# A two-layer decoder on one core: first attention in a fixed TensorE order, norms by powers on GpSimd, and later or earlier turns for experts and gated layer

## The chip, the core and the metric

The kernel runs on one NeuronCore of a Trainium2 chip. TensorE (PE) does matmuls and transposes, VectorE (DVE), ScalarE (ACT) and GpSimd (POOL) the rest, SyncE (SP) issues most of the transfers. The metric is the device time of one execution in microseconds (us); lower is better.

## The reference

The input is x, 16 sequences of 128 tokens with 256 features, and a context of the same shape. Two layers, each of three residual blocks on a layer norm of x:

```python
# layer 0
x = x + attention(ln(x))          # 16 heads of 128, causal, softmax
x = x + wkv(ln(x), ctx)           # a recurrence over the tokens, by channel
h = ln(x)                         # 16 experts of width 176, the top 4 of softmax(h @ router.T)
x = x + sum_top4(w_e * (silu(h@G_e) * (h@U_e)) @ D_e) + sigmoid(h@s) * shared(h)
# layer 1
x = x + rms_attention(ln(x))      # 16 heads of 16
x = x + cross_attention(ln(x), ctx)   # 16 query heads of 128 over 4 key heads
q = act_quant(ln(x))              # rounded to 127 steps of each row's largest
h = silu(q @ tern(Wg).T) * (q @ tern(Wu).T)
x = x + act_quant(h) @ tern(Wd).T # "gated layer": weights of -1, 0, 1; 832 wide
```

## The kernel before

Rows of 128 tokens are called tiles; four tiles make a group g. x stays in SBUF throughout. PE, DVE, ACT and POOL each work through a queue in order. Which instruction stands where in a queue is set by the program's order and by a planner that may reorder within its bounds; inside a `manual_schedule(engines={ET})` PE's own order is the program's.

**First attention** (8 to 648 us). A unit is one tile and four heads: 64 units. `pipeline` runs a step per unit with the stages `scores` (scores `sc`, the causal mask by a POOL affine select, `projv`, the softmax), `values` two steps later (`z`), `ahead` (the q and k projections `proj` of the next four heads; the norm of the next group, `norm0`), `project_out` three steps later (`acc_l`), `turn` one step later (`pT`, and its copy `probT`). The fifth stage, `between`, issues up to two waiting scatters and takes four turns of the generator `wkv_and_route`: when a group's attention is done, its wkv block and routing run in pieces beside the next group's units. A `yield` ends a piece. wkv takes the norm of four tiles (`norm_stats`, `norm_T`: the rows `hrow`, eight transposes `lnT`), works on the two halves of the features with DVE scans, ACT exponentials and POOL products, and adds its result to x by transposes `addb`. `route` takes the norm `hg`, the logits, the top four, and a place in the expert's list `hs` in DRAM; 16 POOL scatters per group (`scatter`) write the rows there. The last group's wkv and route run beside the shared expert.

**Shared expert** (650 to 784 us): 24 units of `pg`, `pu`, `acc_sh`.

**Routed experts** (784 to 1055 us): 79 tiles of 128 list rows. Per step s the loop issues `fetch(s)`, `turn_in(s-2)` (transposes `pht`), `inner(s-3)` (`pgu`, and on DVE `eact`), `turn_act(s-4)` (transposes `pat`, copied by DVE to `eactT`), `outer(s-LAG)` (`pey`, written back to `hs`), and `beside(s)`: loads, the rounding of the gated layer's weights, the gathers of finished rows, and from step FIRST on the first pieces of layer 1. `pht`, `pgu`, `pat` and `pey` share the PSUM pool `tps` with four buffers.

**Layer 1** (1055 us to the end): 64 slots, four to a batch of one tile, in a manual PE order. Each step u issues `scores(u)`, `query_sums(u+1)`, `pieces(early)`, `project_out(u-3)`, `query_norms(u+1)`, `values(u-2)`, `project(u+2)`, `pieces(late)`, `turn(u-1)`, `pieces(last)`. The tables early, late and last name by slot which pieces of the first layer-1 attention (`sa_...`, up to six batches ahead) and of the gated layer (`ff_...`, batches behind) go there. The gated layer's pieces are `ff_start` (norm and rounding, `xqq`), `ff_first_T` (`xqpT`), `inner0` and `inner1` (`pg`, `pu`, the hidden rows `hh`, and after inner1 the rounding to `hqq`), `ff_second_T` (`hqpT`) and `ff_outer` (`py`, the result to DRAM). `ends` and the final loop place those of the last batches.

**Norms.** In layer 0 1/sqrt is an ACT Sqrt and a DVE reciprocal (`rsqrt`); in layer 1 it is a POOL power with the exponent -0.5 (`power`).

Of the kernel before, what the change touches and what calls it, by code (L numbers as in the profile page):

```python
# [17 lines left out]
P = 128  # L18
B = 16
# [33 lines left out]
def decoder(ctx, tc, a, out):  # L53
# [58 lines left out]
    V.memset(zeros_b, 0.0)  # L112
    eps = {}
    for e in (LN_EPS, ATT_EPS, RMS_EPS):
        eps[e] = const.tile([P, 1], F32, tag=f"eps{len(eps)}", name=f"eps{len(eps)}")
        V.memset(eps[e], e)
    warm = const.tile([P, 1], F32, name="warm")
    A.activation(warm, eps[LN_EPS], AF.Sqrt)

# [3 lines left out]

    def rsqrt(pool, src, shape, eps_, tag, scale=1.0):
        r = pool.tile(list(shape), F32, tag=tag, name=tag)
        A.activation(r, src, AF.Sqrt, bias=eps[eps_], scale=scale)
        V.reciprocal(r, r)
        return r

    def norm_stats(pool, g):  # L130
        st = pool.tile([P, G, 6], F32, tag="bnst", name="bnst")
        mv = pool.tile([P, G, 2], F32, tag="bnmv", name="bnmv")
        for t in range(G):
            V.bn_stats(st[:, t, :], xt[g * G + t])
            V.bn_aggr(mv[:, t, :], st[:, t, :])
        return mv, rsqrt(pool, mv[:, :, 1], [P, G], LN_EPS, "rstd")

    def norm_rows(pool, g, t, mv, scale, bufs=2):
        h = pool.tile([P, D], F32, tag="hrow", name="hrow", bufs=bufs)
        V.tensor_scalar(h, xt[g * G + t], mv[:, t, 0:1], scale[:, t : t + 1], ALU.subtract, ALU.mult)  # L140
        return h

    def norm_T(pool, g, mv, scale, dst, bufs=2, psum="main"):

        pts = [ps4("lnT", psum) for _ in range(NK)]
        for t in range(G):
            h = norm_rows(pool, g, t, mv, scale, bufs)
            for k in range(NK):
                PE.transpose(pts[k][:, t, :], h[:, k * P : (k + 1) * P], ident)
        for k in range(NK):  # L150
            nc.any.tensor_copy(dst(k), pts[k])

    def layernorm_T(pool, g, bufs=2, psum="main"):
        hT = pool.tile([P, NK, GT], F32, tag="hT", name="hT")
        mv, rstd = norm_stats(pool, g)
        norm_T(pool, g, mv, rstd, lambda k: hT[:, k, :].rearrange("p (t s) -> p t s", t=G), bufs, psum)
        return hT

# [10 lines left out]
    def heads_out(acc, t, zT, w, h0, last):  # L169
# [6 lines left out]
        return ins.ins  # L176

    def add_back(g, yT, gate=None):

        for t in range(G):  # L180
            pb = ps1("addb")
            for k in range(NK):
                PE.transpose(pb[:, k * P : (k + 1) * P], yT[:, k, t * S : (t + 1) * S], ident)
            x = xt[g * G + t]
            if gate is None:
                V.tensor_tensor(x, x, pb[:, :D], ALU.add)
            else:
                V.scalar_tensor_tensor(x, pb[:, :D], gate[:, t : t + 1], x, ALU.mult, ALU.add)

# [63 lines left out]
    behind = []  # L253

    def wkv(g, psum):

# [6 lines left out]
        yield  # L263
        norm_T(wkp, g, mv, rstd, lambda k: kp[k][:, :, 1:], 2, psum)
        yield
        for k in range(NK):
# [51 lines left out]
            V.tensor_tensor(y, aa0, bb0, ALU.mult)  # L318
            for _ in range(5):
                yield  # L320
            pb = ps4("addb", psum)
# [78 lines left out]
    def route(g, psum):  # L400
# [10 lines left out]
        hg = rt.tile([P, G, D], F32, tag="hg", name="hg")  # L411
        pts = [ps4("lnT", psum) for _ in range(NK)]
        yield
        for t in range(G):
            V.tensor_scalar(hg[:, t, :], xt[g * G + t], mv[:, t, 0:1], rstd[:, t : t + 1], ALU.subtract, ALU.mult)
            for k in range(NK):
                PE.transpose(pts[k][:, t, :], hg[:, t, k * P : (k + 1) * P], ident)
        yield
        hT = rt.tile([P, NK, GT], F32, tag=f"hT{g}", name=f"hT{g}")
        for k in range(NK):  # L420
            nc.any.tensor_copy(hT[:, k, :].rearrange("p (t s) -> p t s", t=G), pts[k])
        routed_T[g] = hT
        yield
        plg = pools[psum].tile([P, G, 32], F32, tag="ps", name="plg")
# [59 lines left out]
        gtb = small("gtb", [P, G, E], BF16)  # L484
        V.tensor_copy(gtb, gt)
        pc = pools[psum].tile([P, 2, G, E], F32, tag="ps", name="pcnt")
        for j, w in ((0, "before"), (1, "ones_b")):
# [51 lines left out]
    with tc.tile_pool(name="l0", bufs=2, reuse_waits="tile") as wk0:  # L539
        hTs, qTs, kTs, live, accs = {}, {}, {}, {}, {}  # L540
        side, last_pool = [], []
# [9 lines left out]

        def norm0(g):
            hTs[g] = layernorm_T(wk0, g, 2, "side")

# [36 lines left out]
        def ahead(u):  # L591

            g, hq, t = place(u)
            if hq == NQ - 2 and t == 0 and g + 1 < NG:
                with tc.issue_after(softmax.last):
                    norm0(g + 1)
            if hq == 0 and t == 2:
                add_bias(g)
            if (u // G + 1) < NG * NQ:
                project(*place(u + G)[:2], t)  # L600
# [32 lines left out]

        norm0(0)
        bias_rows()
        for i in range(4):
            project(0, 0, i)
        pipeline(
            NG * NQ * G,
            [(scores, 0), (values, 2), (ahead, 0), (project_out, 3), (turn, 1), (between, 0)],  # L640
        )
    psum0.close()
# [82 lines left out]

    ET, SPE = mybir.EngineType.PE, mybir.EngineType.SP
    why = "the map holds each of its candidates once"
# [224 lines left out]
    U = B * NKV  # L952
    mhalf = xa.tile([P, 2 * H], F32, name="mhalf")
    GP.memset(mhalf, -0.5)

    def power(v, n):

        power.last = GP.tensor_tensor(v, v, mhalf[:, :n], ALU.pow).ins  # L958

    def flat2(v):  # L960
# [193 lines left out]

    hurried = {}

    def pieces(table, u):
        b, n = divmod(u, NKV)
        for f, ahead in table[n]:
            if 0 <= b + ahead < B - hurried.get(f, 0):  # L1160
                f(b + ahead)
# [19 lines left out]

    LAG, FIRST, APART = 5, 35, 2
    GATHER = TOPK + E - 1 + LAG + 2
# [302 lines left out]
    hurried.update({ff_start: 2, ff_first_T: 2, inner0: 2, inner1: 2, ff_second_T: 3, ff_outer: 3})  # L1486
# [7 lines left out]
    def unit(f, u):  # L1494
        if 0 <= u < U:
            f(u)


# [4 lines left out]
    with tc.manual_schedule(engines={ET}):  # L1503
        keys(0)
        project(0)
        project(1)
        query_sums(0)
        values_in(0)
        query_norms(0)
        keys_T(0)  # L1510
        keys(1)
        for u in range(U + 3):
            unit(scores, u)
            unit(query_sums, u + 1)
            pieces(early, u)
            unit(project_out, u - 3)
            unit(query_norms, u + 1)
            unit(values, u - 2)
            unit(project, u + 2)
            pieces(late, u)  # L1520
            unit(turn, u - 1)
            pieces(last, u)
            for f, n in ends.get(u, ()):
                f(B - n)
# [45 lines left out]
```

## Time and profile before

| What | us |
|---|---|
| median of 3 runs | 1710.32 (1708.59 to 1715.99) |
| the profiled execution | 1719.15 |
| its span | 1717.5 |
| PE busy | 1635.2 |
| DVE busy | 957.8 |
| ACT busy | 839.2 |
| POOL busy | 546.6 |
| PE clock, mean | 0.984 |

A span is the time from the first to the last instruction of the profiled execution. Rows give an engine, the source line, the operation with its tiles (out<-in), and the idle time ahead of it with what ended that. POOL's powers of layer 1 are at line 958, the Sqrt of layer 0 at line 126; the layer-0 scatters are at line 520.

### The profile page before, as it was taken

The page shows a single profiled execution, that of the slowest core. Times are in us where ns is not written, and L with a number is a line of the kernel's source. Part 1 is how long each engine was busy: PE and PEld are TensorE (multiplying, and loading weights), DVE is VectorE, ACT ScalarE, POOL GpSimd, SP SyncE. Part 2 cuts the span into 40 slices and gives each one's busy share as a digit, 9 for nine tenths or more (in the row PEclk, how much of TensorE's full clock was granted, in tenths as well). Part 3 has the DMA queues.
Part 4 walks back from the last instruction along what each step waited for, and adds up shares of the span by engine and source line. Part 5 has one row for each costly group of instructions (what it writes and reads, how often), then busy time and mean ns, then how long its engine had stood idle before and what let it go on. Part 6 is the DMA issues. An engine that isn't in the chain of part 4 may idle for free.

```text
span 1717.5 us, 27384 instructions
## 1 busy us (share of the span) xinstructions
PE 1635.2 (95%) x9824; PEld 1149.0 (67%) x9824; DVE 957.8 (56%) x2522; ACT 839.2 (49%) x2229; POOL 546.6 (32%) x554
## 2 busy tenths in 40 slices
PE   8999999999998988999999999899999999999995
PEld 4666656656665665556676667677777777777773
DVE  2333675375538457613345555467666666666664
ACT  4454545455444534212434445565665666555552
POOL 1010221241124042211146345644444444323320
PEclk9999999999999999999999999999999999999996
DMA  9990000000000019213353235000000000000000
GB/s 294 396 344 1 1 13 1 31 25 7 6 32 25 1 50 251 82 40 102 111 151 116 93 91 171 28 4 8 7 8 7 8 7 10 7 8 7 4 7 10
DMA packets 91646, 110.24 MB, mean 64 GB/s; under 512 B 8630, under 2 KB 66934, under 8 KB 91510
## 3 DMA queue, kind: packets, MB, share of 16 engines
q1 hardware_dynamic: 83078, 89.55, 16.0%
q0 software_dynamic: 6144, 16.79, 3.2%
q10 hardware_dynamic: 2288, 2.14, 0.4%
q8 instruction: 79, 1.29, 0.3%
q14 instruction: 57, 0.47, 0.1%
HBM read 54.06 MB, written 54.39 MB: 63 GB/s over the span
## 4 chain that ended last, share of the span: by engine, by line
PE 78%; issue 7%; DVE 7%; POOL 4%; ACT 3%; DMA 1%; POOLq 0%; ACTq 0%; DVEq 0%; SPq 0%
PE proj L563 11%; PE proj L1309 6%; PE acc_x L1374 6%; PE projv L582 5%; PE acc_l L172 5%; PE pgu L912 4%; PE pey L935 3%; PE sc L1339 3%; PE z L611 3%; PE sc L573 3%; PE z L1359 3%; PE pg L698 2%; PE acc_sh L716 2%; PE pu L698 2%; PE pkv L1051 1%
## 5 line engine op out<-in xcount | busy, mean ns | idle before, releaser
L199 ACT ACTIVATE sc<-sc,nmax 128x128 f32<-128x128 f32 x512 | 199.2, 390 | 183.9 <-DVE nmax L196 150.4
L196 DVE TENSOR_REDUCE nmax<-sc 128x4 f32<-128x512 f32 x128 | 87.3, 682 | 191.6 <-POOL sc L576 188.4
L576 POOL TENSOR_SCALAR_AFFINE_SELECT sc<-sc 128x512 f32<-128x512 f32 x64 | 42.9, 670 | 378.1 <-ACT sc L575 352.3
L1309 PEld LDWEIGHTS proj<-hc,wbig 128*128 128x128 f32 x1024 | 125.3, 194 | 34.0 <-issue 22.0
L1309 PE MATMUL proj<-hc,wbig 128*128 128x128 f32 x1024 | 126.2, 277 | 4.2 <-DVE sc L1342 3.9
L958 POOL TENSOR_TENSOR rq<-rq,mhalf 128x4 f32<-128x4 f32 x64 | 66.8, 1043 | 194.9 <-DVE rq L1332 178.8
L582 PE MATMUL projv<-wv,hT 128*128 128x512 f32 x256 | 123.1, 603 | 5.9 <-DVE v L587 4.6
L1374 PE MATMUL acc_x<-wbig,zT 128*128 128x256 f32 x512 | 126.0, 389 | 0.0
L563 PE MATMUL proj<-hT,wq 128*128 128x512 f32 x256 | 124.7, 609 | 0.0
L172 PE MATMUL acc_l<-wo,zT 128*128 128x256 f32 x512 | 121.6, 380 | 0.0
L172 PEld LDWEIGHTS acc_l<-wo,zT 128*128 128x128 f32 x512 | 96.4, 190 | 37.4 <-issue 27.1
L563 PE MATMUL proj<-hT,wk 128*128 128x512 f32 x256 | 121.0, 593 | 0.0
L912 PE MATMUL pgu<-wbig,hxT 128*128 x316 | 109.6, 470 | 4.5 <-DVE eactT L928 3.2
L1374 PEld LDWEIGHTS acc_x<-wbig,zT 128*128 128x128 f32 x512 | 94.2, 192 | 23.1 <-issue 11.3
L958 POOL TENSOR_TENSOR ss<-ss,mhalf 128x32 f32<-128x32 f32 x16 | 87.1, 5442 | 43.8 <-DVE ss L1060 43.8
L1342 DVE SCALAR_TENSOR_TENSOR sc<-sc,rq,mask 128x128 f32<-128x128 f32 x256 | 77.9, 342 | 35.9 <-PE sc L1339 21.4
L611 PEld LDWEIGHTS z<-probT,v 128*128 128x128 f32 x512 | 67.5, 194 | 44.1 <-issue 26.2
L199 ACT ACTIVATION_READ_ACCUMULATOR sc<-sc,nmax 128x1 f32 x512 | 95.7, 187 | 0.0
L1169 POOL DMA_INDIRECT back<-hs,idx x64 | 63.6, 993 | 93.3 <-DMA hs<-ey 75.5
L563 PEld LDWEIGHTS proj<-hT,wk 128*128 128x128 f32 x256 | 48.4, 191 | 59.4 <-issue 50.3
L928 DVE COPY eactT<-pat 88x256 f32<-88x256 f32 x79 | 33.0, 418 | 91.7 <-PE pat L926 68.1
L1345 POOL TENSOR_TENSOR sc<-sc,rsum 128x512 f32<-128x512 f32 x64 | 66.9, 1046 | 50.0 <-DVE rsum L1344 18.6
(352 smaller groups left out, 3538.6 us busy)
## 6 DMA issues: line engine op xcount, KB each, us to landing
hs<-zero SPq DMA_DIRECT2D x16, 2048.0 KB
hx<-hs SPq DMA_DIRECT2D x79, 128.0 KB
hs<-ey SPq DMA_DIRECT2D x79, 128.0 KB
wbig<-in_L_ffn_w_gate_dram SPq DMA_DIRECT2D x2, 1408.0 KB
wbig<-in_L_ffn_w_up_dram SPq DMA_DIRECT2D x2, 1408.0 KB
wd<-in_L_ffn_w_down_dram SPq DMA_DIRECT2D x2, 1408.0 KB
x<-in_x_dram SPq DMA_DIRECT2D x4, 512.0 KB
wq<-in_L_attn_W_Q_dram SPq DMA_DIRECT2D x8, 256.0 KB
```

The lines of the kernel that those rows point to most:

```text
L172: ins = PE.matmul(acc[:, t, :], zT[:, i, :], w[:, h0 + i, :], start=False, stop=last and i == 3, skip_group_check=True,)
L196: softmax.last = V.tensor_reduce(nmax, sc, AX.X, ALU.max, negate=True).ins
L199: A.activation(p[:, i, :], sc[:, i, :], AF.Exp, bias=nmax[:, i : i + 1], accum_out=rs[:, i : i + 1])
L563: PE.matmul(pj, w[:, k, h, :], hTs[g][:, k, :], start=k == 0, stop=k == NK - 1)
L582: PE.matmul(pv, hTs[g][:, k, at], wv[:, k, 4 * hq : 4 * hq + 4, :].rearrange("p h e -> p (h e)"), start=k == 0, stop=k == NK - 1,)
L611: PE.matmul(pz[:, i, :], v[:, i, :], pT[:, i, :], start=True, stop=True)
L698: ins = PE.matmul(d[c * HP : c * HP + cols.stop - cols.start, :n], w[:, k, cols], routed_T[g][:, k, c * n : (c + 1) * n], start=k == 0, st ...
L912: PE.matmul(pg, hT[:, k, :], wgu[:, k, bass.ds(held[j], 1), :].rearrange("p e i -> p (e i)"), start=k == 0, stop=k == NK - 1,)
L958: power.last = GP.tensor_tensor(v, v, mhalf[:, :n], ALU.pow).ins
L1309: PE.matmul(pj[:, i, :], wqx[:, n, k, i * DH : (i + 1) * DH], hTs[b][:, k, :], start=k == 0, stop=k == NK - 1,)
L1342: V.scalar_tensor_tensor(sc[:, i, :], psc[:, i, :], rq[:, i : i + 1], mask, ALU.mult, ALU.add)
L1374: PE.matmul(accs[b][:, :D], zT[:, i, :], wox[:, 4 * n + i, :], start=n == 0 and i == 0, stop=n == NKV - 1 and i == 3,)
```

## The change

- PE's order in first attention is that of the program. `norm0` is spread over three steps; `hrow` has four buffers.
- `rsqrt` goes; `norm_stats` uses a DVE add and `power`.
- The generator takes four turns (`a_unit`) between wkv's rows and their transposes, between route's rows and their transposes, between those and the logits, and ahead of the counts `pcnt`; four instead of five ahead of `addb`.
- Experts: `turn_act` at lag 5, LAG 6, FIRST 36.
- Gated layer: ff_start in slot 2 (was 3), ff_first_T in 3 (was 0 of the next batch), inner0 in 0 (was 1), inner1 in 1 (was 2), ff_second_T in 2 (was 0 of the next batch), ff_outer in 3 (was 1 of the next batch). The pieces of batch 14 are placed in the last steps by the stage that they follow, and those of batch 15 and the last ff_outer calls behind the loop.

```diff
-    def rsqrt(pool, src, shape, eps_, tag, scale=1.0):
-        r = pool.tile(list(shape), F32, tag=tag, name=tag)
-        A.activation(r, src, AF.Sqrt, bias=eps[eps_], scale=scale)
-        V.reciprocal(r, r)
-        return r
+    def power(v, n):
+        power.last = GP.tensor_tensor(v, v, mhalf[:, :n], ALU.pow).ins
...
-        return mv, rsqrt(pool, mv[:, :, 1], [P, G], LN_EPS, "rstd")
+        r = pool.tile([P, G], F32, tag="rstd", name="rstd")
+        V.tensor_scalar_add(r, mv[:, :, 1], LN_EPS)
+        power(r, G)
+        return mv, r
...
+    def a_unit():
+        for _ in range(4):
+            yield
...
-        norm_T(wkp, g, mv, rstd, lambda k: kp[k][:, :, 1:], 2, psum)
+        hs = norm_rows(wkp, g, mv, rstd)
+        yield from a_unit()
+        norm_T(hs, lambda k: kp[k][:, :, 1:], psum)
...
-            for _ in range(5):
-                yield
+            yield from a_unit()
             pb = ps4("addb", psum)
...
-            if hq == NQ - 2 and t == 0 and g + 1 < NG:
+            if hq == NQ - 2 and t < 3 and g + 1 < NG:
                 with tc.issue_after(softmax.last):
-                    norm0(g + 1)
+                    norm0(g + 1, t)
...
-        pipeline(
-            NG * NQ * G,
-            [(scores, 0), (values, 2), (ahead, 0), (project_out, 3), (turn, 1), (between, 0)],
-        )
+        with tc.manual_schedule(engines={ET}):
+            pipeline(
+                NG * NQ * G,
+                [(scores, 0), (values, 2), (ahead, 0), (project_out, 3), (turn, 1), (between, 0)],
+            )
...
-    LAG, FIRST, APART = 5, 35, 2
+    LAG, FIRST, APART = 6, 36, 2
...
-                for f, lag in ((fetch, 0), (turn_in, 2), (inner, 3), (turn_act, 4), (outer, LAG)):
+                for f, lag in ((fetch, 0), (turn_in, 2), (inner, 3), (turn_act, 5), (outer, LAG)):
...
-        [(load_context, 2), (norm_rows_x, 1), (keys_T, 1), (ff_first_T, -2), (ff_second_T, -3)],
-        [(norm_T_x, 1), (inner0, -2), (ff_outer, -3)],
-        [(values_in, 1), (inner1, -2)],
-        [(row_stats, 2), (ff_start, -1)],
+        [(load_context, 2), (norm_rows_x, 1), (keys_T, 1), (inner0, -2)],
+        [(norm_T_x, 1), (inner1, -2)],
+        [(values_in, 1), (ff_second_T, -2), (ff_start, -1)],
+        [(row_stats, 2), (ff_outer, -2), (ff_first_T, -1)],
...
     ends = {
-        U - 2: [(ff_start, 2)],
-        U - 1: [(ff_second_T, 3), (ff_first_T, 2), (inner0, 2), (ff_outer, 3), (inner1, 2)],
-        U: [(ff_second_T, 2)],
-        U + 1: [(ff_outer, 2)],
+        (U - 1, "turn"): [ff_start],
+        (U, "project_out"): [ff_first_T, inner0],
+        (U, "values"): [inner1],
+        (U + 1, "values"): [ff_second_T],
     }
...
-        for f in hurried:
+        for f in (ff_start, ff_first_T, inner0, inner1):
             f(B - 1)
+        ff_outer(B - 2)
+        ff_second_T(B - 1)
+        ff_outer(B - 1)
```

More of the change, by code (lines that the diff above doesn't have):

```diff
@@ L112, in decoder @@
     V.memset(zeros_b, 0.0)
[L113 to L118, printed above, removed]
+    mhalf = const.tile([P, 2 * H], F32, name="mhalf")
+    GP.memset(mhalf, -0.5)
+    ET, SPE = mybir.EngineType.PE, mybir.EngineType.SP
     tdecay = vector_load("L0_xattn_time_decay", [P, NK])
     tfirst = vector_load("L0_xattn_time_first", [P, NK])
-    def rsqrt(pool, src, shape, eps_, tag, scale=1.0):
-        r = pool.tile(list(shape), F32, tag=tag, name=tag)
-        A.activation(r, src, AF.Sqrt, bias=eps[eps_], scale=scale)
-        V.reciprocal(r, r)
-        return r
+    def power(v, n):
+        power.last = GP.tensor_tensor(v, v, mhalf[:, :n], ALU.pow).ins
     def norm_stats(pool, g):
@@ L135, in norm_stats, with norm_rows, norm_T, by_tiles @@
             V.bn_aggr(mv[:, t, :], st[:, t, :])
-        return mv, rsqrt(pool, mv[:, :, 1], [P, G], LN_EPS, "rstd")
[L138 to L143, printed above, removed]
+        r = pool.tile([P, G], F32, tag="rstd", name="rstd")
+        V.tensor_scalar_add(r, mv[:, :, 1], LN_EPS)
+        power(r, G)
+        return mv, r
+    def norm_rows(pool, g, mv, scale):
+        hs = []
+        for t in range(G):
+            h = pool.tile([P, D], F32, tag="hrow", name="hrow", bufs=G)
+            V.tensor_scalar(h, xt[g * G + t], mv[:, t, 0:1], scale[:, t : t + 1], ALU.subtract, ALU.mult)
+            hs.append(h)
+        return hs
+    def norm_T(hs, dst, psum):
         pts = [ps4("lnT", psum) for _ in range(NK)]
         for t in range(G):
-            h = norm_rows(pool, g, t, mv, scale, bufs)
             for k in range(NK):
-                PE.transpose(pts[k][:, t, :], h[:, k * P : (k + 1) * P], ident)
+                PE.transpose(pts[k][:, t, :], hs[t][:, k * P : (k + 1) * P], ident)
         for k in range(NK):
             nc.any.tensor_copy(dst(k), pts[k])
[L153 to L157, printed above, removed]
+    def by_tiles(hT, k):
+        return hT[:, k, :].rearrange("p (t s) -> p t s", t=G)
     def rows_accumulator(name):
@@ L176, in heads_out @@
         return ins.ins
[L178 to L188, printed above, removed]
     def last_dim(v, n):
@@ L411, in route @@
         hg = rt.tile([P, G, D], F32, tag="hg", name="hg")
-        pts = [ps4("lnT", psum) for _ in range(NK)]
         yield
@@ L415, in route @@
             V.tensor_scalar(hg[:, t, :], xt[g * G + t], mv[:, t, 0:1], rstd[:, t : t + 1], ALU.subtract, ALU.mult)
-            for k in range(NK):
-                PE.transpose(pts[k][:, t, :], hg[:, t, k * P : (k + 1) * P], ident)
-        yield
+        yield from a_unit()
         hT = rt.tile([P, NK, GT], F32, tag=f"hT{g}", name=f"hT{g}")
-        for k in range(NK):
-            nc.any.tensor_copy(hT[:, k, :].rearrange("p (t s) -> p t s", t=G), pts[k])
+        norm_T([hg[:, t, :] for t in range(G)], lambda k: by_tiles(hT, k), psum)
         routed_T[g] = hT
-        yield
+        yield from a_unit()
         plg = pools[psum].tile([P, G, 32], F32, tag="ps", name="plg")
@@ L485, in route @@
         V.tensor_copy(gtb, gt)
+        yield from a_unit()
         pc = pools[psum].tile([P, 2, G, E], F32, tag="ps", name="pcnt")
@@ L539, in decoder @@
     with tc.tile_pool(name="l0", bufs=2, reuse_waits="tile") as wk0:
-        hTs, qTs, kTs, live, accs = {}, {}, {}, {}, {}
+        hTs, qTs, kTs, live, accs, norms = {}, {}, {}, {}, {}, {}
         side, last_pool = [], []
@@ L550, in bias_rows, with norm0 @@
             V.tensor_copy(bo_row, pb[:, :D])
-        def norm0(g):
-            hTs[g] = layernorm_T(wk0, g, 2, "side")
+        def norm0(g, part):
+            if part == 0:
+                norms[g] = norm_stats(wk0, g)
+            elif part == 1:
+                norms[g] = norm_rows(wk0, g, *norms[g])
+            else:
+                hTs[g] = wk0.tile([P, NK, GT], F32, tag="hT", name="hT")
+                norm_T(norms.pop(g), lambda k: by_tiles(hTs[g], k), "side")
         def add_bias(g):
@@ L632, in between @@
                     side.pop(0)
-        norm0(0)
+        for part in range(3):
+            norm0(0, part)
         bias_rows()
@@ L724, in sh_down @@
                 V.scalar_tensor_tensor(xt[b], acc[:, t, :], sg[:, b : b + 1], xt[b], ALU.mult, ALU.add)
-    ET, SPE = mybir.EngineType.PE, mybir.EngineType.SP
     why = "the map holds each of its candidates once"
@@ L952, in decoder @@
     U = B * NKV
[L953 to L958, printed above, removed]
     def flat2(v):
@@ L1153, in decoder @@
     last = ([(row_stats, 6)], [(sa_scale, 6)], [(sa_rows, 6), (sa_split, 5)], [])
-    hurried = {}
+    apart = {}
     def pieces(table, u):
@@ L1159, in pieces @@
         for f, ahead in table[n]:
-            if 0 <= b + ahead < B - hurried.get(f, 0):
+            if 0 <= b + ahead < B - apart.get(f, 0):
                 f(b + ahead)
@@ L1485, in decoder, with unit @@
     early[3].append((keys, 2))
-    hurried.update({ff_start: 2, ff_first_T: 2, inner0: 2, inner1: 2, ff_second_T: 3, ff_outer: 3})
+    for f in (ff_start, ff_first_T, inner0, inner1, ff_second_T, ff_outer):
+        apart[f] = 2
     ends = {
-        U - 2: [(ff_start, 2)],
-        U - 1: [(ff_second_T, 3), (ff_first_T, 2), (inner0, 2), (ff_outer, 3), (inner1, 2)],
-        U: [(ff_second_T, 2)],
-        U + 1: [(ff_outer, 2)],
+        (U - 1, "turn"): [ff_start],
+        (U, "project_out"): [ff_first_T, inner0],
+        (U, "values"): [inner1],
+        (U + 1, "values"): [ff_second_T],
     }
-    def unit(f, u):
+    def unit(f, u, step=None):
         if 0 <= u < U:
             f(u)
+        for f_ in ends.get((step, f.__name__), ()):
+            f_(B - 2)
     late_backs = {
@@ L1515, in decoder @@
             pieces(early, u)
-            unit(project_out, u - 3)
+            unit(project_out, u - 3, u)
             unit(query_norms, u + 1)
-            unit(values, u - 2)
+            unit(values, u - 2, u)
             unit(project, u + 2)
             pieces(late, u)
-            unit(turn, u - 1)
+            unit(turn, u - 1, u)
             pieces(last, u)
-            for f, n in ends.get(u, ()):
-                f(B - n)
             if u in late_backs:
```

## The prediction

> **What bounds the kernel now.** The page first: TensorE (PE) is busy for 95% of the span and DVE for 56%, so the time is PE's work plus the holes in it. The second line shows that PE ran at full clock except in a few slices, above all the last.
>
> ```profile
> PE 1635.2 (95%) x9824; PEld 1149.0 (67%) x9824; DVE 957.8 (56%) x2522; ACT 839.2 (49%) x2229; POOL 546.6 (32%) x554
> ...
> PEclk9999999999999999999999999999999999999996
> ```
>
> Then the windows by stage (length, PE, weight loads, DVE, ACT, POOL, clock, DMA): first attention, shared expert, routed experts, steady gated layer, end.
>
> ```profile
> 8.00:648.00 640.00, 617.73 (x2728) 401.98 (x2728) 332.60 (x691) 309.65 (x833) 139.26 (x168) 0.99 0.23 80
> 650.00:784.00 134.00, 127.99 (x478) 72.53 (x477) 68.36 (x148) 35.83 (x50) 29.40 (x33) 0.99 0.40 111
> 784.00:1055.00 271.00, 255.26 (x1545) 184.56 (x1544) 130.78 (x364) 115.21 (x293) 107.84 (x95) 0.99 0.39 122
> 1106.00:1548.00 442.00, 441.78 (x3763) 346.64 (x3761) 294.50 (x912) 267.82 (x734) 193.35 (x164) 1.00 0.02 7
> 1662.00:1717.50 55.50, 33.30 (x158) 20.51 (x156) 28.40 (x87) 17.79 (x43) 4.17 (x5) 0.75 0.03 10
> ```
>
> First attention lacks 22.3 us, the routed experts 15.7, the end 22.2; the steady gated layer lacks 0.2 in 442: there the change can only lose. Third, what PE waits for (total, times, longest):
>
> ```profile
> PE hqpT L1409 <- ACT hqq L847: 12.8, 3, 4.9
> PE z L611 <- ACT probT L212: 10.8, 8, 2.1
> ...
> PE pat L926 <- DVE eact L919: 5.6, 6, 2.0
> PE xqpT L1409 <- ACT xqq L847: 4.7, 1, 4.7
> PE projv L582 <- DVE v L587: 4.6, 1, 4.6
> ...
> PE pgu L912 <- DVE eactT L928: 3.2, 2, 2.5
> ```
>
> PE's work is the same in both kernels, so I price holes. A hole also costs clock: after the 2.07 us wait of z at 391.5 the window 392.6 to 396.0 shows clock 0.51, so 3.4 us do 1.7 us of work.
>
> **Norms.** Per norm of four tiles ACT's Sqrt (297 ns) and DVE's reciprocal (177) become a DVE add (0.15) and a GpSimd pow; the row of that pow, 128x4, is 1043 ns. Only at the start does PE wait for it (lnT, 5.9 us): 1.19 for 0.47, **+0.7**. Eleven table loads of 1283 ns leave ACT at Sqrt, about as many at the Exp behind it; in the steady units PE waits for none of them, so I give them 0. The Trainium skill (GPSIMD Engine Reference, 4.1 Engine selection) advises VectorE, not GpSimd, for elementwise work; our rows agree, and what decides is the place in GpSimd's queue.
>
> **First attention, groups 1 to 3.** The wkv transposes now stand between units, four turns behind what feeds them, and no longer inside proj. What stalls z is different: ACT's copy probT stands behind Exps that wait for GpSimd (1.84 and 1.18 us, L290 and L304), and these stay. The zones cost 5.4, 5.7 and 5.7 us, the last two with 1.7 of clock. Laying the new order out with the same durations gives 5.1, 7.0 and 7.0, one hole of 2.8 in each of the last: **+1** (-4 to +5).
>
> **End of first attention.** With three more waits of four turns, route(2) ends later. Before, eight of its scatters go ahead of one causal mask on GpSimd; that is the 4.57 us wait of projv:
>
> ```profile
> 612.08 0.63 POOL L576 TENSOR_SCALAR_AFFINE_SELECT sc<-sc 128x512 f32<-128x512 f32 x1 [8.59 <-DVE cnt L499]
> 615.00 1.02 POOL L520 DMA_INDIRECT hs<-hg,idx  x1 [2.28 <-DVE idx L513]
> ...
> 624.30 0.96 POOL L520 DMA_INDIRECT hs<-hg,idx  x1 [0.30 <-issue]
> 625.28 0.64 POOL L576 TENSOR_SCALAR_AFFINE_SELECT sc<-sc 128x512 f32<-128x512 f32 x1
> ```
>
> In the changed program all 16 come behind the last mask, then the pow of wkv(3), which DVE's hrow and PE's eight lnT need, and those lnT precede the first pg of the shared expert. At 1.27 us apart the scatters take 20.3 us, pow 1.0, hrow 0.4, lnT 1.6: 23.3 us after the last mask. Before, PE worked for 11.7 us from there (636.7 to 648.4). So PE idles for 11.6, plus 1.7 of clock: 13.3. Gone are 4.57 and its clock (6.8 us at 0.50: 3.4), and 1.34 at pg falls into the hole: 9.3. **+4** (-2 to +9: if pow came early nothing is idle, if the hole costs two slow stretches 1.7 more). The skill (TensorE: Matmul & The Clock Gate, "Why this matters for your kernels") says that holes over some 3 us halve the clock; it speaks against this edit. Our row shows it from 2.07; by the rule alone the 2.8 us holes above would stay at full clock.
>
> **Shared expert.** The wkv and route pieces come a little later; laid out again, 6.5 us of holes and 1.7 of clock as before. Scatters end before unit 24, so the first fetch stays covered. **0** (-3 to +3).
>
> **Experts' second turn.** turn_act goes from lag 4 to 5, a step between eact and its transposes. It should end the wait of pat (5.6) and part of pgu's (3.2). But one step takes four tiles of the PSUM pool tps, whose four buffers go round, and in the changed program pat takes the buffer that the pgu of one step ago held: it waits until DVE has read that for the *next* eact. So PE waits for an eact one step old, as before; pgu waits for the eactT of one step ago in both. **0** (-9 to +3; -9 if those waits did vanish).
>
> **Gated layer, steady.** inner1 goes to slot 1, second_T to slot 2: one slot from pu to hqpT where there were two. Rows of before for the pieces:
>
> ```profile
> 1249.98 0.60 PE L1067 MATMUL pqT<-ident,spread 128*128 128x128 f32 x4
> ...
> 1251.97 1.02 DVE L1389 TENSOR_REDUCE hqst<-hh 128x1 f32<-128x832 f32 x1
> 1254.19 0.64 DVE L845 TENSOR_SCALAR hh<-hh,hqsc 128x832 f32<-128x832 f32 x1
> ...
> 1256.30 0.88 ACT L847 ACTIVATE hqq<-hh 128x832 bf16<-128x832 f32 x1
> ```
>
> From the end of pu: slot 2's sc ends at 1.0, acc_x at 4.2. On DVE, in the changed order, hh ends at 2.1, its maximum 3.2, x+acc_x 4.6, nmax 5.4, scaling 5.9, rounding 6.7. On ACT z's copy and four Exps (5.9 to 7.4) stand ahead of hqq, which ends at 8.3. hqpT's place is 8.9 (by PE's rows from sc to pv): 0.6 to spare. Next is pqT, at 9.5: it needs spread, and on DVE spread now stands behind hrow of ff_start, which needs the rstd pow (0.56) behind rq's pow (1.04): 8.6, then hrow, rstd, spread to 9.7. A hole of 0.2 in some ten batches: **+2** (0 to +20, where the chain takes 1.5 us longer in all 14).
>
> **End.** From slot 62 the ends of batch 14 are spread over the steps. In before hqpT waits 4.94 and 3.10 ahead of the last x, with 10.2 us at half clock (5.1 lost). Laid out, the new order has holes of 2.8 and 3.3 and one stretch less at half clock (1.7), and outer(14), 0.9, moves into the idle tail: 8.04 - 6.1 + 1.7 + 0.9 = 4.5. The chain of batch 15 after the last x (20.0 us, 1697.5 to 1717.5) stays. **-4.5** (-7.5 to -1). Slots of 7.9 us before that, where batches have no first-layer pieces, are shorter than the 8.3 above: 0.4 in two or three, **+1** (0 to +3). The entry of this layer keeps its order: 0 (-3 to +3).
>
> **Sum.** 0.7 + 1 + 4 + 0 + 0 + 2 + 1 - 4.5 = +4.2. The profiled execution took 1719.15 (span 1717.5 and 1.65 around it) and would be 1723.4; it lies 8.8 above the median of its three runs, so 1710.32 + 4.2 = 1714.5. Runs of this kernel can tell about 0.5%, 8.55 us, from no change.
>
> **Rivals.**
> - Slower: the gated layer's DVE and ACT chain. One slot instead of two leaves 0.6 us; from 2 us more (say hqq behind one more late Exp, or the rstd pow behind the 1.04 us pow of the sc rows) PE stands 1.5 us in each of 14 batches: 21, so 1735. For it: in the thin slots at the end the same wait is before's largest (12.8). Against it: the durations above are steady to 1%. 0.22.
> - Faster: the last wkv's pow comes before the scatters have blocked GpSimd (the 13.3 shrinks to 4 or less), or the second turn does free the experts' PE (-9). Either gives about 1705 and both 1696; with z's holes in the zones (10.8 us) gone as well, under 1690. For it: the waits named are real. Against it: the order of GpSimd's queue and the buffer. 0.26.
> - The change does not do what it says: all parts are covered by other work but the L0 end, whose gain and loss cancel: 1710, no change. 0.08.
> - The forecast: 1706 to 1724, 0.44.
>
> By the bounds 1701.8 and 1718.9: of the forecast 0.28 same, 0.14 slower, 0.02 faster; of the faster rival 0.16 faster, 0.10 same; neutral is same, the slower rival slower: faster 0.18, same 0.46, slower 0.36. The range from 1699 to 1732 leaves out the upper part of the slower rival and the lower of the faster.
>
> **What would show it.** At the end of first attention the wait of projv is gone and PE idles some 12 us, ended by hrow, with 16 scatters in a row ahead of a pow: without that hole the L0 step is wrong. Among the experts the waits of pat and pgu on DVE keep about their 9 us; if they fall under 3, the buffer step is wrong. From 1106 to 1548 the steady layer shows holes at pqT of some tenths; holes over 1 us at hqpT are the slower rival. The two waits of hqpT ahead of the last x fall to about 6 together.

## The result and the profile after

| | before | after |
|---|---|---|
| median, us | 1710.62 (1708.59 to 1715.99, 4 runs) | 1741.35 (1741.14 to 1741.96, 4 runs) |
| ratio | | 1.0175 [1.0152, 1.0199] |
| profiled execution, us | 1719.15 | 1741.96 |
| its span, us | 1717.5 | 1740.3 |

The ratio is that of the times, with its 95% interval in brackets. The change costs 30.7 us, by the medians; the forecast was +4.2 and the range ended at 1732. The two profiled executions differ by only 22.8: before's stood 8.5 above its median, after's 0.6. So 22.8 can be placed by comparing the traces, and 8 are a question about the base.

First the page of after: the span, the engines, the clock that was granted.

```profile
span 1740.3 us, 27352 instructions
...
PE 1642.0 (94%) x9824; PEld 1157.4 (67%) x9824; DVE 970.5 (56%) x2514; ACT 807.1 (46%) x2198; POOL 551.2 (32%) x566
...
PEclk9999999999999998999999999999999999999997
```

PE has the same 9824 instructions. One slice has lost clock (the sixteenth, 653 to 696 us); the last one is a little better. Now the windows of after by stage, with the columns of the windows of before: length, PE, weight loads, DVE, ACT, POOL, clock, DMA.

```profile
8.00:648.00 640.00, 618.01 (x2730) 402.82 (x2730) 339.52 (x687) 285.06 (x808) 141.45 (x183) 0.99 0.23 79
650.00:784.00 134.00, 120.77 (x431) 70.08 (x432) 68.67 (x143) 30.43 (x43) 35.26 (x37) 0.92 0.41 119
784.00:1055.00 271.00, 258.33 (x1549) 186.04 (x1548) 126.69 (x355) 114.44 (x292) 108.46 (x95) 0.98 0.38 114
1106.00:1548.00 442.00, 428.11 (x3593) 334.62 (x3586) 290.40 (x887) 249.77 (x693) 183.87 (x159) 1.00 0.02 7
1662.00:1740.00 78.00, 58.31 (x344) 41.18 (x342) 45.18 (x140) 34.67 (x96) 12.81 (x14) 0.89 0.02 8
```

In the steady gated layer PE stood for 0.2 us of 442 before and now stands for 13.9, at full clock. The second window starts with the idle end of first attention (13.2 lacking, clock 0.92). What PE waits for, in after (total, times, longest):

```profile
PE lnT L149 <- DVE hrow L140: 20.5, 3, 11.5
PE z L606 <- ACT probT L197: 15.6, 10, 2.6
PE pqT L1056 <- DVE spread L1061: 10.1, 10, 2.0
PE hqpT L1398 <- ACT hqq L843: 9.9, 3, 4.0
...
PE pey L931 <- DVE eactT L924: 3.9, 2, 3.7
...
PE scT L1097 <- DVE hh L1435: 3.3, 10, 0.3
...
PE pgu L908 <- DVE eactT L924: 2.4, 1, 2.4
...
PE py L1453 <- DVE nm L1082: 1.6, 9, 0.2
...
PE pat L922 <- DVE eact L915: 1.2, 1, 1.2
```

Three waits of the list come in nine or ten batches where before had them once (pqT, 0.9) or not at all (scT and py). To see what they cost, take the end of PE's last instruction of each piece in the two traces; how much later it comes in after, and the step from one to the next (acc_x is layer 1's output projection, 32 matmuls in a batch):

| Landmark (end) | before | after | later by | step | forecast |
|---|---|---|---|---|---|
| first lnT (start) | 8.32 | 8.85 | 0.5 | +0.5 | +0.7 |
| last acc_l | 648.37 | 647.50 | -0.9 | -1.4 | -7 |
| first pg (start) | 649.71 | 660.69 | 11.0 | +11.9 | +12 |
| last acc_sh | 783.83 | 793.20 | 9.4 | -1.6 | 0 |
| last pey | 1052.19 | 1059.27 | 7.1 | -2.3 | 0 |
| acc_x of batch 1 | 1161.32 | 1171.79 | 10.5 | +3.4 | 0 |
| acc_x of batch 11 | 1568.16 | 1596.43 | 28.3 | +17.8 | +2 |
| acc_x of batch 14 | 1666.22 | 1693.75 | 27.5 | -0.8 | +1 |
| acc_x of batch 15 | 1697.42 | 1719.47 | 22.1 | -5.4 | -4.5 in all |
| span's end | 1717.5 | 1740.3 | 22.8 | +0.7 | |

The steps add up to 22.8. The step of 17.8 and 2.6 of the 3.4 ahead of it (the way from batch 0 to batch 1) are the gated layer, and that is where the forecast went most wrong. By batches of the steady part: 41.60 us each before, 43.70 after.

**The place of the loss.** This is the timeline of after in slot 2 of a steady batch (start, length, engine, line, instruction, and idle time ahead of it with what ended that). spread holds the scaled q and k rows of the first layer-1 attention, and pqT is PE's transpose of them in sa_split.

```profile
1305.80 1.01 POOL L123 TENSOR_TENSOR rq<-rq,mhalf 128x4 f32<-128x4 f32 x1 [8.48 <-DVE rq L1321]
...
1306.78 0.55 POOL L123 TENSOR_TENSOR rstd<-rstd,mhalf 128x1 f32<-128x1 f32 x1
...
1307.30 1.04 POOL L1334 TENSOR_TENSOR sc<-sc,rsum 128x512 f32<-128x512 f32 x1
...
1307.36 1.12 DVE L971 TENSOR_SCALAR hrow<-x,bnmv,rstd 128x256 f32<-128x256 f32 x1 [0.81 <-POOL rstd L123]
...
1308.48 0.68 DVE L1061 TENSOR_TENSOR spread<-qk,ss 128x512 f32<-128x512 f32 x1
...
1309.21 0.66 PE L1056 MATMUL pqT<-ident,spread 128*128 128x128 f32 x4 [0.91 <-DVE spread L1061]
```

The rstd power ends at 1307.3, 8.5 after the end of pu where the prediction's walk has 8.6, from rq's power through rstd's. Then hrow, priced at 0.4, takes 1.12 and ends 0.14 after GpSimd's sc multiply, which started 0.06 ahead of it. The rows of all hrow of the steady part (min/median/max in ns), before and after, show that this length is not its own:

```profile
L982 DVE TENSOR_SCALAR hrow<-x,bnmv,rstd x30: 398/404/414, 1120.8 to 1545.2; 128x256 f32<-128x256 f32 x30
```

```profile
L971 DVE TENSOR_SCALAR hrow<-x,bnmv,rstd x30: 396/404/1124, 1110.6 to 1542.7; 128x256 f32<-128x256 f32 x30
```

In the whole trace of after 13 hrow start while an sc multiply is under way (nine of them in this row), and all 13 take 1.12; the others of the row take 0.40 to 0.41, also beside a power. So spread is late, and pqT. In other slots PE waits for PSUM; the last row is scT in before, in one piece:

```profile
1320.42 1.03 PE L1453 MATMUL py<-wdq,hqT 128*128 128x256 bf16 x7 [0.18 <-DVE nm L1082]
...
1334.46 0.55 PE L1097 MATMUL scT<-q2T,kT 32*128 32x128 f32 x6
...
1335.35 1.15 PE L1097 MATMUL scT<-q2T,kT 32*128 32x128 f32 x26 [0.33 <-DVE hh L1435]
```

```profile
1315.41 1.17 PE L1108 MATMUL scT<-q2T,kT 32*128 32x128 f32 x32
```

scT has nothing to do with hh, nor py with nm. But the pool of the wide PSUM tiles gives its four buffers out in turn: scT needs those that inner0's hh is read from, and inner0 now stands right ahead of it. The idle time in these rows is only a part of what is lost, since the six matmuls ahead of the gap are drawn out too. Measured from the start of each piece on PE to the start of the next, a batch grows by 0.99 in the stretch of hqpT, which ends where pqT can start, by 0.87 in that of scT, by 0.34 in that of pT, which ends with py's wait, and by -0.1 elsewhere: the 2.1.

**The end of first attention** in after, the scatters of the last group (the first and the last of the 16), the power and the norm's transposes:

```profile
636.95 1.04 POOL L508 DMA_INDIRECT hs<-hg,idx  x1 [2.29 <-DVE idx L501]
...
656.34 0.96 POOL L508 DMA_INDIRECT hs<-hg,idx  x1 [0.30 <-issue]
...
657.31 1.05 POOL L123 TENSOR_TENSOR rstd<-rstd,mhalf 128x4 f32<-128x4 f32 x1
...
658.95 1.94 PE L149 MATMUL lnT<-ident,hrow 128*128 128x128 f32 x8 [11.45 <-DVE hrow L140]
```

It is the predicted picture: 16 scatters, the power behind them, a hole of 11.45, and 13.7 us at half clock from 650.5.

### The profile page after: what moved, and what is told of

The parts are those of the page before. It is cut to its first block, busy times and chain, and to the rows that moved or that the text cites. A ratio compares the mean times of both kernels' runs of the same rounds, so it can differ in the third digit from the quotient of the medians.

```text
span 1740.3 us, 27352 instructions
## 1 busy us (share of the span) xinstructions
PE 1642.0 (94%) x9824; PEld 1157.4 (67%) x9824; DVE 970.5 (56%) x2514; ACT 807.1 (46%) x2198; POOL 551.2 (32%) x566
## 4 chain that ended last, share of the span: by engine, by line
PE 73%; DVE 13%; ACT 5%; issue 4%; POOL 4%; DMA 1%; ACTq 0%; POOLq 0%; SPq 0%; DVEq 0%
PE proj L558 11%; PE proj L1298 5%; PE acc_l L169 5%; PE projv L577 5%; PE acc_x L1363 5%; PE pgu L908 5%; PE pey L931 4%; PE z L606 3%; PE sc L568 3%; PE z L1348 2%; PE sc L1328 2%; PE acc_sh L713 2%; PE pg L695 2%; PE pu L695 2%; PE pk L1264 2%
## 5 line engine op out<-in xcount | busy, mean ns | idle before, releaser
L1363 PEld LDWEIGHTS acc_x<-wbig,zT 128*128 128x128 f32 x512 | 93.5, 190 | 23.1 <-issue 11.3
L931 PE MATMUL pey<-wd,eactT 88*128 x316 | 83.2, 386 | 4.8 <-DVE eactT L924 3.9
## 6 DMA issues: line engine op xcount, KB each, us to landing
hs<-zero SPq DMA_DIRECT2D x16, 2048.0 KB, 18.6
```

The source lines that it names most:

```text
L931: ins = PE.matmul(py, aT[:, k, :], wd[:, bass.ds(held[j], 1), k, :].rearrange("p e d -> p (e d)"), start=k == 0, stop=k == 1,)
L1363: PE.matmul(accs[b][:, :D], zT[:, i, :], wox[:, 4 * n + i, :], start=n == 0 and i == 0, stop=n == NKV - 1 and i == 3,)
```

## Experiments

Two theories after the result. A: the loss has two places, the steady gated layer (hrow behind the sc multiply, and PSUM buffers) and the power behind the scatters. B, the rival: it is spread, in that PE's fixed order and the later turns leave less slack everywhere, or the experts' turn takes part in it. The median of before was 1711 in the first comparison, 1719 to 1721 in the next three, on three chips, and 1711 in the last, on a fourth. So each run is put beside the runs of before made with it. The whole change itself was run only on chips where before takes 1711.

**One part at a time.** Each is before with one part of the change alone.

ff_alone: the order of the gated layer, and its ends.

```diff
-        [(row_stats, 2), (ff_start, -1)],
+        [(values_in, 1), (ff_second_T, -2), (ff_start, -1)],
+        [(row_stats, 2), (ff_outer, -2), (ff_first_T, -1)],
...
+        (U + 1, "values"): [ff_second_T],
```

> The kernel before with the gated layer's part alone (its new slots, its new ends). Theory A (the loss sits in the steady gated layer: a batch of four slots takes 43.70 us after and 41.60 before): about 10 batches x 2.1 = +20, less 5 to 6 at the end, so +13 to +17 us against before. Rival B (the loss is made at the end of first attention and shows later only because stages shift): -5 to 0.

Measured: 1741.49 beside 1721.29, 1.0112 [1.0093, 1.0130], +20.2, above the 13 to 17 expected; a steady batch takes 43.71. The gated layer alone brings all of the 2.1 a batch. From acc_x of batch 14 to the end it takes 49.9, where before takes 51.3 and after 46.6, so here the new ends gave less than in the whole.

l0_alone: fixed order, powers, turns between rows and transposes.

```diff
-        return mv, rsqrt(pool, mv[:, :, 1], [P, G], LN_EPS, "rstd")
+        power(r, G)
...
+        with tc.manual_schedule(engines={ET}):
```

> The kernel before with the first attention's part alone (TensorE order, powers on GpSimd, four-turn waits). Theory A: +9 to +12 us, from the 11.5 us hole ahead of lnT at the end of first attention, less what the projv wait gives back; the zones neutral. Rival B: +20 or more.

Measured: 1735.78 beside 1721.29, 1.0070 [1.0046, 1.0093], +14.5; the hole at lnT 11.54, a steady batch 41.60. That is more than expected; 4.45 us of it is a wait of acc_sh for DVE's act at 763.55 that neither profile of the whole change has. DVE and ACT stand there too, 6.7 us each, for nothing that the trace shows on this core; mended (below) has the same at 767.89, 5.13. What makes it is open.

moe_alone: turn_act at lag 5, LAG 6, FIRST 36.

```diff
-    LAG, FIRST, APART = 5, 35, 2
+    LAG, FIRST, APART = 6, 36, 2
```

> The kernel before with the experts' part alone (turn_act at lag 5, LAG 6, FIRST 36). Theory A: -3 to 0 us; pat waits for the eact of the next tile because of its PSUM buffer, so the step more gains little, and what leaves pat and pgu comes back at pey. Rival C (the step more does cover eact): -6 to -9 us.

Measured: 1721.74 beside 1721.29, 1.0006 [0.9991, 1.0021]: nothing. The parts add up to 35.2 (20.2 + 14.5 + 0.5) and the whole costs 29 to 31, so they don't simply add; but B's third place is excluded on this chip, to within the interval of some 3.6 us.

before_again: before, unchanged, once more.

> The kernel before, unchanged, for a second profile: its first profiled execution was 8.8 us above the median of its runs. If that was one slow stretch, this span is near 1709 and one stage is shorter by most of 8.8; if profiling itself costs it, the span is again near 1717.

Measured: 1723.83, span 1722.1. The stage of the routed experts takes 268.4 us in the first profile of before and 270.3 in this one, by the landmarks last acc_sh to last pey, from the same code. The median here is 1721, so the run does not decide where the 8.8 of the first profile come from.

**The steady gated layer.** Four variants of after.

split_first: first attention's sa_rows and sa_split go ahead of hqpT's piece and ff_start in slot 2, so that spread stands ahead of hrow on DVE.

```diff
+    last[2][:] = [(values_in, 1), (sa_rows, 6), (sa_split, 5), (ff_second_T, -2), (ff_start, -1)]
```

> The changed kernel with sa_rows and sa_split moved ahead of ff_second_T and ff_start in slot 2, so that spread no longer stands behind ff_start's hrow on DVE. Theory A (pqT waits for spread, spread for hrow, and hrow takes 1.12 us instead of 0.40 while GpSimd multiplies the sc rows): pqT's hole of 0.9 us falls under 0.2, a steady batch takes 42.7 to 42.9 us instead of 43.70. Rival (PE waits at hqpT or for a PSUM buffer there, and the hole moves to hqpT): 43.5 to 43.7.

Measured: 1735.85 beside 1719.02; a batch takes 42.77, as expected, and pqT no longer waits. That is 0.93 of the 2.1. hrow itself still takes 1.12 behind the multiply; PE only no longer needs what stands behind it.

psum_order: inner0 goes to the head of its slot's late pieces, and ff_outer with ff_first_T ahead of sa_scores.

```diff
+    late[0][:0] = [(inner0, -2)]
+    late[3][:0] = [(ff_outer, -2), (ff_first_T, -1)]
```

> The changed kernel with inner0 moved to the head of slot 0's late pieces and ff_outer and ff_first_T ahead of sa_scores in slot 3; all else stays. Theory A (scT takes four PSUM buffers of the pool wide and waits 0.87 us for those that DVE reads for s and hh; py waits 0.35 us for one that DVE reads for nm): 43.70 falls by 1.0 to 1.25, to 42.45 to 42.7 a batch, and pqT's hole stays at 0.9. Rival (PE waits for the data of scT and py, or the trace shows something that costs nothing): 43.5 to 43.7.

Measured: 1739.12 beside 1719.02; a batch takes 43.18, short of the 42.45 to 42.7 expected. scT (1.10) and the group of py (1.80) are back at before's lengths, but 0.73 of it returned at the sc of sa_scores, which now takes the buffers of py and xqpT (1.83 from its start to the next piece, 1.10 in before and after):

```profile
1317.48 0.29 PE L1398 MATMUL xqpT<-ident_b,xqq 128*128 128x128 bf16 x2
...
1317.70 1.90 PE L1079 MATMUL sc<-kT,qT 16*128 16x128 f32 x32
```

both_orders: both edits.

> The changed kernel with both moves above. Theory A: 41.5 to 41.8 us a batch, as before the change, and 20 us less than the changed kernel in all; about +8 to +13 against the kernel before. Rival (a third wait shows up in their place): 42.5 or more a batch.

Measured: 1734.08 beside 1719.02, 1.0088 [1.0067, 1.0109]; a batch takes 42.24, between the two theories: 0.64 over before, and 0.73 stands at that sc.

sc_in_four: the sc multiply on GpSimd as four of 128x128.

```diff
-        GP.tensor_tensor(sc, sc, last_dim(rs, S), ALU.mult)
+        for i in range(4):
+            GP.tensor_tensor(sc[:, i, :], sc[:, i, :], rs[:, i : i + 1].to_broadcast([P, S]), ALU.mult)
```

> The changed kernel with GpSimd's multiplication of the layer-1 sc rows (128x512, 1.04 us) issued as four of 128x128. Theory A (DVE's hrow cannot start, or stands still, while GpSimd's multiplication holds what both read through): hrow waits for one quarter only, its row falls from 1.12 to 0.4 to 0.75 us and pqT's hole from 0.9 to 0.2 to 0.6. Rival (hrow is long because of its own scalar operand, rstd, fresh from GpSimd): hrow stays at 1.12.

The row of hrow in this kernel, with the columns of the one above:

```profile
L971 DVE TENSOR_SCALAR hrow<-x,bnmv,rstd x29: 402/481/517, 1119.5 to 1532.0; 128x256 f32<-128x256 f32 x29
```

The longest hrow falls from 1124 to 517 ns, pqT's wait from 0.91 to 0.48, a batch to 43.27; hrow and the wait lie where theory A had them: hrow waits for the multiply that is under way, not for the amount of GpSimd's work, and not for its fresh rstd, which is the same here. The whole took 1747.71 beside 1719.02 in one execution, with 272 us in the routed experts; only the batch is read.

**The end of first attention.**

scatters_behind: after, with the last group's scatters issued behind wkv(3)'s power, two to a unit.

```diff
-        some_scatters(len(scatters))
+        some_scatters(2 if len(steps) == 2 else len(scatters), power.last)
```

> The changed kernel with the 16 scatters of group 2 issued behind wkv(3)'s power instead of ahead of it (two per unit of the shared expert). Theory A (the 11.5 us hole at lnT is GpSimd's queue: 16 scatters of 1.27 us ahead of a 1.05 us power): the hole falls to 3 to 4.5 us (add to x, statistics, power, hrow), less time at half clock, so first pg comes 7 to 11 us sooner; some of it may return in the shared expert, where wkv now waits for the scatters: -4 to -10 against the changed kernel in all. Rival (the hole is made by DVE or by the last x): it stays over 8 us.

Measured: 1755.89 beside 1720.79, 1.0208 [1.0188, 1.0228]: +35.1, where after itself has +29.0 and +30.7 on other chips and a gain of 4 to 10 was expected. Its timeline, PE in the shared expert and GpSimd:

```profile
650.39 1.57 PE L149 MATMUL lnT<-ident,hrow 128*128 128x128 f32 x8 [3.75 <-DVE hrow L140]
...
657.69 0.96 POOL L508 DMA_INDIRECT hs<-hg,idx  x1 [0.31 <-issue]
...
658.67 1.29 POOL L282 TENSOR_TENSOR e2b<-kp,pp 128x512 f32<-128x512 f32 x1
...
665.03 3.58 PE L713 MATMUL acc_sh<-wsh,act 128*128 128x256 f32 x8 [4.61 <-DVE act L703]
...
675.82 3.52 PE L713 MATMUL acc_sh<-wsh,act 128*128 128x256 f32 x8 [3.67 <-DVE act L703]
...
696.41 3.46 PE L713 MATMUL acc_sh<-wsh,act 128*128 128x256 f32 x8 [4.12 <-DVE act L703]
```

The hole at lnT falls from 11.45 to 3.75, and the first pg comes 9 us sooner. But the scatters now stand ahead of wkv's products on GpSimd, DVE waits 8.34 us for one of them with act queued behind, and PE stands three times in the shared expert; the third wait, 4.12, after has as well (4.11 at 693.53), the other two are new. The hole was moved, and by the last acc_sh 6.2 are lost against after.

hold_scatters: before, with the group's scatters held until the last mask is issued.

```diff
-            some_scatters(2, last_pool[0])
+            if u < NG * NQ * G - 8:
+                some_scatters(2, last_pool[0])
```

> The kernel before with the scatters of group 2 held until the last causal mask has been issued. Theory A (in before, eight scatters ahead of one mask cost 4.57 us at projv and 3.4 us of clock): -6 to -9 us against before, and projv's wait is gone. Rival (the scatters then hold up wkv(3) on GpSimd, as in the changed kernel): -2 to +3.

Measured: 1719.85 beside 1720.79, 0.9998 [0.9984, 1.0012]. The wait of projv is gone and the last acc_l ends 6.9 and 8.3 sooner than in the two profiles of before; then pg waits 4.41 for DVE's last x, the first pg is 3.8 and 5.2 sooner, the last acc_sh 0.6 and 1.3. Of the 6 to 9 expected nothing is left at the end: the rival's range.

**Several edits together.**

mended: after, with scatters_behind, split_first, inner0 at the head of its slot, and ff_outer with ff_first_T behind keys in early of slot 3, where sa_scores' buffers are not in use.

```diff
+    early[3].extend([(keys, 2), (ff_outer, -2), (ff_first_T, -1)])
```

> The changed kernel with the scatters behind the power, sa_split first, inner0 at the head of slot 0's late pieces, and ff_outer and ff_first_T ahead in slot 3 (in the early pieces, so that sa_scores finds free PSUM buffers). Theory A (queues and the four buffers of wide are all of the loss): a steady batch 41.6 to 41.8 us; against the kernel before between -3 and +6. Rival (something else was lost too): +10 or more against before.

Measured: 1743.18 beside 1720.79, 1.0144 [1.0107, 1.0182], +22.4 where -3 to +6 was expected: the rival's side. Its window of the steady part (same columns as above):

```profile
1150.00:1548.00 398.00, 397.29 (x3400) 311.76 (x3398) 277.51 (x841) 232.35 (x649) 174.67 (x148) 1.00 0.03 8
```

PE lacks 0.7 in 398, and a batch takes 41.57: the gated layer's loss is gone, and the sc of sa_scores is back at its length:

```profile
1327.36 1.17 PE L1079 MATMUL sc<-kT,qT 16*128 16x128 f32 x32
```

What stays is in the shared expert, which ends 20.5 later than in before: behind the hole of 3.75 at lnT four waits for DVE's act of 3.65 to 5.13.

ff_mended: before with the gated layer's part in these orders, and the new ends; first attention and experts as in before.

> The kernel before with the changed gated layer in the mended orders (sa_split first, inner0, ff_outer and ff_first_T early) and the new ends; first attention and experts as before. Theory A: steady batches of 41.57 us, the end shorter: -3 to -6 us against before, where the same part in the change's own order gave +20. Rival: 0 or more.

Measured: 1710.81 beside 1711.07, 0.9989 [0.9979, 1.0000]; a batch takes 41.57. The part that cost 20.2 costs nothing in this order, but the gain of 3 to 6 that was expected did not come. Its profiled execution gives the best view of how the stage of the routed experts varies; the windows of before and of ff_mended from 784 us to the end of the last pey, rounded:

```profile
784.00:1052.00 268.00, 252.26 (x1518) 181.58 (x1517) 128.74 (x359) 114.21 (x291) 107.56 (x94) 0.99 0.39 119
```

```profile
784.00:1046.00 262.00, 250.66 (x1519) 181.78 (x1519) 129.54 (x359) 113.85 (x291) 108.58 (x94) 0.99 0.39 122
```

The same instructions within a few recorded ones, in 262 instead of 268 us: 15.7 us without PE against 11.3, the waits of pht for hxT not among them this time.

best: before with hold_scatters and the mended gated layer.

> The kernel before with the held scatters and the changed gated layer in the mended orders (sa_split first, inner0, ff_outer and ff_first_T early) and the new ends. Theory A: steady batches of 41.6 to 41.8, the end 3 to 6 us shorter, the projv wait gone: -8 to -14 us against before. Rival: the thin slots or a new PSUM wait give it back: -5 to +2.

Measured: 1718.45 beside 1720.79, 0.9989 [0.9973, 1.0005], a batch 41.57: not to be told from before, where -8 to -14 was expected.

after_again: after, unchanged, once more.

> The changed kernel, unchanged, beside the kernel before on one more chip. The parts alone gave +20.2 (gated layer), +14.5 (first attention) and 0 (experts), in all more than the profiles of the two whole kernels show (span +22.8, or +18.1 against before's second profile). Theory A (the shared expert and the experts' entry differ from execution to execution, the rest does not): +18 to +25 us. Rival (the parts add, or the first comparison's +30.7 holds everywhere): +28 to +35.

Measured: 1740.08 beside 1711.07, 1.0165 [1.0148, 1.0182], +29.0; the hole at lnT is 11.48. The size of the loss repeats at 29 to 31, with before again at 1711, as the rival had it.

sqrt_back: after, with Sqrt and reciprocal in layer 0 in place of add and power.

```diff
-        V.tensor_scalar_add(r, mv[:, :, 1], LN_EPS)
-        power(r, G)
+        A.activation(r, mv[:, :, 1], AF.Sqrt, bias=eps, scale=1.0)
+        V.reciprocal(r, r)
```

> The changed kernel with layer 0's norms by Sqrt on ACT and reciprocal on DVE again; the order of first attention and all else stays changed. Theory A (the hole at lnT is there because the norm of wkv(3) goes through GpSimd behind 16 scatters): no hole over 5 us at the end of first attention, first pg 8 to 11 us sooner, -8 to -12 us against the changed kernel. Rival (the fixed order alone makes the hole): -3 to +1.

Measured: 1736.45 beside 1711.07, 1.0136 [1.0119, 1.0153]: 3.6 less than after_again, where 8 to 12 less was expected. Its timeline, PE:

```profile
651.01 1.96 PE L697 MATMUL pg<-hT,wsh 128*128 128x512 f32 x4 [1.42 <-DMA wsh<-in_L_ffn_sh_gate_dram]
...
680.71 0.63 PE L317 MATMUL addb<-ident,y 128*128 128x128 f32 x4 [2.53 <-DVE y L312]
...
696.91 0.94 PE L162 MATMUL acc_sh<-zeros_b 1*128 1x512 bf16 x2 [3.40 <-DVE x L723]
```

The hole at lnT is gone and pg starts at 651.01 (after: 660.69), so the power behind the scatters is its cause. Waits of 1.65 to 3.40 in the shared expert take about 5 back, and at the start the first lnT comes at 10.98, 1.7 later than in after_again.

sqrt_and_moves: the same with the mended gated layer.

> The changed kernel with Sqrt and reciprocal in layer 0 and the gated layer in the mended orders. Theory A (the change's own two losses taken out): the projv wait of before is gone, steady batches 41.57, the end shorter: -6 to -14 us against before. Rival (the fixed order costs what it saves): -4 to +3.

Measured: 1719.45 beside 1711.07, 1.0042 [1.0026, 1.0059], +8.4; expected was a gain. The new order of first attention with Sqrt still ends the shared expert 3.3 later than in ff_mended on the same chip, the start 2.6 of that; a further 4.5 is in the experts' stage (266.7 against 262.3). Whether the later turns make that, or this execution, is open. No version was measurably faster than before; ff_mended and best equal it, where after is 29 to 31 us slower.

## Why the prediction was wrong, step by step

The forecast's sum was +4.2, and 22.8 was found between the profiles: 18.6 off. By the landmarks it is 17.4 in the gated layer (20.4 where 3 stood), 3.7 in first attention up to the last acc_sh (9.4 where 5.7 stood), -2.3 in the experts and -0.2 at the end. A further 8 come from the base.

- **Gated layer, steady: the step that failed.** "A hole of 0.2 in some ten batches: +2". The mechanism at pqT was right: spread behind hrow, hrow behind rstd's power, that behind rq's, and the power's end fits the walk to 0.1 us. The term hrow was mis-sized: 0.4 from a row where GpSimd was not multiplying, 1.12 here, so that PE waited 0.91 a batch at pqT where 0.2 stood. The Trainium skill (SBUF — State Buffer, "Who interferes with whom") says that VectorE's faster two-port modes and GpSimd hold a port pair as a lock for a whole instruction, tensor_scalar being one that can enter such a mode, and that whoever starts first blocks the other. The runs agree as far as they go: 13 of 13 that start behind the 1.04 us multiply take 1.12, and with the multiply in quarters none takes over 0.52. Beside a power hrow kept its 0.40. The ports themselves no trace shows. I did not price that overlap.
- **And a term that was not in the sum.** scT (+0.87) and py (+0.34) wait for buffers. The prediction priced the four-buffer pool for the experts, and not for this layer, where inner0 was moved right ahead of scT, and py and xqpT right behind sa_scores. psum_order shows the cause, by giving those back and losing 0.73 at the next user of the pool.
- **The slower rival** had the size: 2.1 in each batch, where it said 1.5. Its mechanism was not the one that came: rstd's power ended on time, and hqpT never waited in the steady part. It was given 0.22, since the walk left 0.6 us of slack at hqpT; the slack was right (hqq ends at 1306.95, hqpT's place is 1307.63) and the next piece was the tight one.
- **End of first attention.** The new hole came, with 11.45 of idle time for "PE idles for 11.6" and 11.9 to the first pg for 12, but the fit is in part luck. The 11.6 holds the 1.6 of the eight lnT, which is no idle time and no new work: before does them too, at 653.25 and 655.40, which fits the step of -1.6 to the last acc_sh. Without them 10.0 of idle time would have been left; the scatters then began 2.29 late, for DVE's idx, which the sum had left out.
- **Ahead of it: -1.4 for some -7.** By the ends of acc_l, unit by unit, after is 2.2 late at unit 16 (the start, priced at 0.7), 4.8 at unit 59, then ahead by 2.1 at unit 60, where projv's wait and its clock are gone (-6.9 for -8.0), and by 0.9 at the last. The three zones so cost 2.6 more where "+1" stood. Their holes were laid out well, 18.9 for 19.1, but 19.1 against before's 16.8 is already +2.3; and three of the four holes of 2.56 and 2.57 were followed by half clock, two of them in the last group. scatters_behind, sqrt_back and hold_scatters show that ending any one of these holes moves half of it or more into the shared expert.
- **Experts: right in the sum, wrong in the detail.** moe_alone is 1.0006. But the waits of pat and pgu on DVE did not keep about 9: together they fell from 8.8 to 3.6 (pat 1.2, pgu 2.4), just over the 3 that the prediction named as its refutation. pey took over 3.9, from nothing, since it needs eactT one step after it is made: the longest wait of pat moved on along the same chain, and by these lists that, not the buffer argument, keeps the sum near 0. The argument itself fails on its own count: at four tiles a step and four buffers in turn, pat comes back, once all stages run, to the buffer of the pat before it, not to pgu's. That the sum is 0 is not shown beyond moe_alone's chip: on the last chip three profiles with the later turns take 265.4 to 266.7 in this stage, ff_mended without them 262.3.
- **End and start: right.** hqpT ahead of the last x waits 3.06 and 2.80, 5.86 for "about 6"; the step is -4.7 for -4.5. The first lnT is 0.5 late for 0.7, though PE is 2.2 late by unit 16 (above). The thin slots gave -0.8 for +1.
- **The base.** The sum was taken from the profiled execution and then lowered by 8.8, as if the change were made to the median. The median is the right base, but then the terms have to be those of a median execution. Where the 8 lie is not shown. The only kernel profiled near 1711 with before's code up to layer 1 is ff_mended; its experts' stage takes 262.3 where before's took 268.4, which would be 6 of the 8. The other kernels with that code take 266.8 to 271.7. The rival is the chip: the record does not name the one of the first profile, and its 1719.15 is near what before takes on three others (1719 to 1721).

What is open: the wait of 4.45 in l0_alone that the whole change lacks, why the experts' stage varies by up to 9 us between executions of the same code, and why the parts add up to 4 to 6 more than the whole.

## What to carry to other kernels

In a layer where PE never stands, price a moved piece at the next two readers of each thing that it takes: the queue in which it lands, the instructions of other engines that run beside it and may lengthen it, and every buffer of a pool that goes round, up to the next user of the pool. Ending one hole ahead of a stage with its own tight chain is worth only what that chain lets through; follow it to the next landmark where both kernels must meet before adding it to a sum. Take base and profile from the same chip and a median execution: where the profile lies 0.5% over the median, as here, the terms and the base do not belong together.

## What the runs showed of the hardware

- A DVE tensor_scalar of 128x256 takes 0.40 us alone or beside a GpSimd power of 128x1 or 128x4, and 1.12 when a GpSimd multiply of 128x512 (1.04) has started ahead of it (13 of 13 in after); with the multiply in four parts, 0.48 to 0.52 (sc_in_four).
- A scatter of 128 rows from GpSimd takes 0.96 and 0.30 to the next: 16 of them hold its queue for some 20 us, and a power of 128x4 behind them still takes 1.05.
- The same program had medians of 1719, 1721 and 1721 us on three chips and 1711 on a fourth; comparisons are sound only within one of them.
